# One division for both heads of a pair, behind the slot's maxima: a decoder layer on one core

## The chip, the cores and the metric

The kernel runs on one core of a Trainium2 chip. The metric is device time in microseconds (us) for one execution of the whole program. Three timed runs of the kernel before gave 662.83, 663.38 and 667.53 us; the median is 663.38 us. One more execution was recorded by the hardware profiler; it took 661.71 us.

## The reference

One decoder layer on x of 4 batches, 1024 rows and 256 features, in float32. Three blocks are added to x one after the other, each on a layer norm of x:

```python
x = x + attn(layernorm(x))          # 16 heads of 16, local: a chunk of 128 rows sees itself and the chunk before, causal
x = x + xattn(layernorm(x), ctx)    # 16 heads of 16, 77 keys from ctx, mask, biases
x = x + ffn(layernorm(x))           # 704 wide, inputs and weights rounded to 8 bits, silu(gate) * up
```

Both attentions are softmax attentions: `softmax(q k^T / 4) v`, then a product with an output matrix. The division of the softmax is by the sum of the exponentials of a row.

## The kernel before, in words

**Layout.** The kernel takes the attention in eight jobs: S0 S1 S2 X0 S3 X1 X2 X3. S is the self attention and X the cross attention of one batch. In a job, g (2) is one half of the features, that is eight heads; these eight heads are two groups of four, o = 0 and o = 1. The four heads of a group (j) lie in the four quarters of 32 partitions, so that TensorE works on four heads at once. A pair of heads here is o = 0 and o = 1 of the same g and j. hf (2) is a half of the 1024 rows. u counts the units of one (g, o): four for S (256 rows each), two for X (512 rows each). A branch is taken at run time, and here the arm runs in which all rows of the mask are alike (`alike` is true).

**Softmax without a second pass.** For each unit the scores are computed twice. First with rows on the partitions (`sc_n`, L735 for S, L750 for X), four PSUM banks, and VectorE takes the row maxima out of them (`maxima`: L765 for S, eight pairs of instructions per unit; L776 for X, four instructions per unit). The maxima are transposed (`ps_mx`, L787), copied (L791) and sent by DMA into a spare row of q (L801). Five units later (`LEAD = 5`) the scores are computed again with keys on the partitions and the maxima already subtracted (`sc_t`, L827 and L856, four banks), and ScalarE takes the exponential (L837, L859). For S, GpSimd sets the masked half to zero (L841).

**Weighted values and the division.** `weighted_values` multiplies the exponentials with the values (`ps_av`, L871 and L881), one bank per (g, o, hf); a column of ones in the values makes the row's sum. VectorE transposes the bank in 32x32 blocks into `o_sb` (L895), which frees the bank. `normalise` takes the reciprocal of the 16 sums (L903) and multiplies 16x16 values (L905) into `aN`, at the place of head o. After o = 1, `by_features` transposes `aN` in 32x32 blocks into `aT` (L917), from which `out_project` (`ps_op`, L306) later computes the product with the output matrix, which VectorE adds to x (L935).

**The order.** It is written out by hand, slot by slot (L1231 to L1290); each engine works through its own list in that order. In a slot come:

1. the weighted values that are due, each with transposition, reciprocal, product and, for o = 1, the transposition to `aT` (L1254 to L1258);
2. usually one task of TensorE from a list ordered by due time: `project` (`ps_p`), `values` (`ps_v`), `normed_T` (`ps_t`, then the copies L341 and L343), `out_project`, preparations of weights;
3. work beside it, mostly VectorE's: statistics of the layer norm (L192, L194), quantising of weights (L608 to L618), the largest values for the next block (L966);
4. `put_maxima`, where a group's maxima were completed one slot before;
5. `sc_n` and the maxima of the unit five ahead;
6. `sc_t`, the exponentials and masks of the unit of this slot.

In a stretch of S units a slot with weighted values is followed by one without; in a stretch of X units each slot has some.

**Banks.** The eight PSUM banks go round in the order in which they are asked for. The first bank that a slot asks for is the one that, eight requests earlier, was the first `sc_n` bank of the slot before (that slot's last eight banks are four `sc_n` and four `sc_t`). So the weighted values at the head of a slot start once VectorE has taken the first bank's maxima in the slot before.

**Buffers.** `o_sb` has one buffer of 128x512, `aN` two, `aT` three, the scratch output `junk` of the maxima two.

Of the kernel before, what the change touches and what calls it, by code (L numbers as in the profile page):

```python
# [9 lines left out]
F32 = mybir.dt.float32  # L10
# [4 lines left out]
ALU = mybir.AluOpType  # L15
# [3 lines left out]
P = 128  # L19
# [6 lines left out]
def decoder_layer(  # L26
# [32 lines left out]
    nc = tc.nc  # L59
# [5 lines left out]
    H, HD, SL = 16, 16, 32  # L65
    NP = 2
    NS = 2
# [3 lines left out]
    HS = S // NH  # L71
# [9 lines left out]
    small = ctx.enter_context(tc.tile_pool(name="small", bufs=3))  # L81
# [120 lines left out]
    with ExitStack() as att:  # L202
# [64 lines left out]
        def slot_of(v, h):  # L267
            return v.rearrange("p h e -> p (h e)")[:, h * (HD + 1) : h * (HD + 1) + SL]
# [7 lines left out]
        def next_of(key, tiles):  # L276
            turn[key] += 1
            return tiles[(turn[key] - 1) % len(tiles)]
# [7 lines left out]
        class Job:  # L286


            def __init__(self, kind, b):
                self.kind, self.b = kind, b  # L290
                self.leads = (kind, b) == ("S", 0)
                self.st = {}
                self.xn, self.xnT, self.vs, self.q, self.k = {}, {}, {}, {}, {}
                self.aN, self.aT, self.mx, self.pts, self.av = {}, {}, {}, {}, {}

            def branch(self):
                twin = copy.copy(self)
                for k, v in vars(self).items():
                    if isinstance(v, dict):
                        setattr(twin, k, dict(v))  # L300
                return twin
# [119 lines left out]
        def attention(alike):  # L421
# [5 lines left out]
            work = arm.enter_context(tc.tile_pool(name="work", bufs=2))  # L427
# [388 lines left out]
            def weights(job, g, o, u):  # L816
# [34 lines left out]
                else:  # L851
# [5 lines left out]
                    for j in range(NJ):  # L857
                        pt = work.tile([SK, HS], F32, name="ptx", tag="pt", bufs=16)
                        nc.scalar.activation(pt, banks[j][:SK], AF.Exp)  # L859
                        job.pts[g, o, j, u] = pt  # L860

            def weighted_values(job, g, o, hf):
                ps = bank("ps_av")
                heads = [2 * NJ * g + 2 * j + o for j in range(NJ)]
                if job.kind == "S":
                    t0 = hf * HT
                    for kb in range(max(t0 - 1, 0), t0 + HT):

                        a0, a1 = max(kb, t0), min(kb + 2, t0 + HT)
                        for j in range(NJ):  # L870
                            nc.tensor.matmul(  # L871
                                ps[j * SL : (j + 1) * SL, (a0 - t0) * P : (a1 - t0) * P],
                                slot_of(job.vs[kb // 2][:, kb % 2], heads[j]),
                                job.pts[g, o, j, kb // 2][:, kb % 2, a0 - kb : a1 - kb, :],
                                start=(kb == max(t0 - 1, 0)),
                                stop=True,
                                skip_group_check=True,
                            )
                else:
                    for j in range(NJ):  # L880
                        nc.tensor.matmul(  # L881
                            ps[j * SL : (j + 1) * SL, :],
                            slot_of(vx[:, job.b], heads[j]),
                            job.pts[g, o, j, hf],
                            start=True,
                            stop=True,
                        )

                if job is jobs[-1] and (g, o, hf) == (NP - 1, NS - 1, NH - 1):
                    job.av[g, o, hf] = next_of("xnT", xnTs)[  # L890
                        :, 0, :
                    ]
                else:
                    job.av[g, o, hf] = work.tile([P, HS], F32, name="o_sb", tag="o_sb", bufs=1)
                nc.vector.transpose(job.av[g, o, hf], ps)  # L895

            def normalise(job, g, o, hf, tail):

                if o == 0:
                    job.aN[g, hf] = work.tile([P, HS], F32, name="aN", tag="aN", bufs=2)  # L900
                on = job.av[g, o, hf].rearrange("p (s e) -> p s e", e=SL)
                rec = small.tile([P, HS // SL, 1], F32, name="rec")
                nc.vector.reciprocal(rec, on[:, :, HD : HD + 1])  # L903
                aN = job.aN[g, hf].rearrange("p (s e) -> p s e", e=SL)
                (nc.gpsimd if tail else nc.vector).tensor_tensor(  # L905
                    aN[:, :, o * HD : (o + 1) * HD],
                    on[:, :, 0:HD],
                    rec.to_broadcast([P, HS // SL, HD]),
                    ALU.mult,
                )  # L910

            def by_features(job, g, o, hf):

                if o == NS - 1:
                    if g == 0:
                        job.aT[hf] = work.tile([P, NC, HS], F32, name="aT", tag="aT", bufs=3)
                    nc.vector.transpose(job.aT[hf][:, g, :], job.aN[g, hf])  # L917
# [181 lines left out]
            jobs = [leading.branch()]  # L1099
# [15 lines left out]
            values_of, added, puts, early, late = {}, {}, {}, {}, {}  # L1115
# [24 lines left out]
            for j, job in enumerate(jobs):  # L1140
# [4 lines left out]
                for hf in range(NH):  # L1145
# [41 lines left out]
                    g = NP - 1  # L1187
# [43 lines left out]
            for slot in range(first, last):  # L1231
                present["slot"] = slot
                now = units[slot] if 0 <= slot < N else None
                ahead = units[slot + LEAD] if 0 <= slot + LEAD < N else None
                for fn, args in early.get(slot, ()):
                    fn(*args)
                tail = slot >= N - LEAD
                if slot == N:

                    pair = values_of[slot] + values_of.pop(slot + 1)  # L1240
                    for args in pair:
                        weighted_values(*args)
                        normalise(*args, tail)
                    for args in pair:
                        by_features(*args)
                    while beside:
                        t = min(beside, key=lambda t: t[1:3])
                        beside.remove(t)
                        t[4](*t[5])
                        while after:  # L1250
                            after.pop(0)()
                    last_project(jobs[-1])
                else:
                    for args in values_of.get(slot, ()):  # L1254
                        weighted_values(*args)
                        normalise(*args, tail)
                        if not tail:
                            by_features(*args)  # L1258
                spent = 0.0
                cap = 1.35 if now and ahead else 2.3  # L1260
                while t := next_in(tasks, slot, spent, cap):
                    spent += t[3]
                    fn, args = t[4:]
                    fn(*args)
                    if fn is out_project:
                        job, hf, t2 = args
                        if job.kind == "X" and t2 == HT // 2 - 1:
                            third_norm(job.b, hf, slot)
                spent = 0.0
                while t := next_in(beside, slot, spent, 1.2):  # L1270
                    spent += t[3]
                    t[4](*t[5])
                if tail and slot < N:
                    for args in values_of.get(slot, ()):
                        by_features(*args)
                for args in puts.get(slot, ()):
                    put_maxima(*args)
                if ahead:
                    max_bias(*ahead)
                    if now and now[0].kind == "X" and not alike:  # L1280
                        weight_bias(*now)
                    maxima(*ahead)
                if now:
                    if alike or not (ahead and now[0].kind == "X"):
                        weight_bias(*now)
                    weights(*now)
                for fn, args in late.get(slot, ()):
                    fn(*args)
                while after:
                    after.pop(0)()  # L1290
# [264 lines left out]
        with tc.If(rows_alike != 0, preferred_fallthrough_block=True) as branch:  # L1555
            attention(True)
            feed_forward()
        with branch.Else():
            attention(False)
            feed_forward()  # L1560
# [49 lines left out]
```

## Time and profile before

| what | value |
|---|---|
| timed runs, median | 663.38 us |
| profiled execution | 661.71 us |
| its span | 660.0 us |
| TensorE busy / VectorE busy, 0 to 548 us (attention) | 525.30 / 447.35 us |
| TensorE busy / VectorE busy, 548 to 660 us (feed forward) | 82.13 / 94.19 us |
| mean granted TensorE clock | 0.986 |

The span is the time between the first and last instruction; the execution took 1.7 us more. PE is TensorE's matmuls, PEld its weight loads, DVE is VectorE, ACT ScalarE, POOL GpSimd, SP the engine that issues DMAs. In a line of the groups of instructions stand the line of the kernel, engine, operation, output <- input, shapes, the count, the busy time in us and the mean time of one in ns, and then the idle time of the engine just before them with what ended it. In the timeline stand the start and the length in us, and in brackets how long the engine had been idle and what it waited for. Busy matmuls are pipelined, four heads beside each other, so their lengths overlap.

### The profile page before, as it was taken

How to read it: one execution, taken by the hardware profiler on the slowest of the kernel's cores; microseconds unless marked ns; L12 is line 12 of the kernel's file. 1: busy time of each engine (PE TensorE's matmuls, PEld its weight loads, DVE VectorE, ACT ScalarE, POOL GpSimd, SP SyncE). 2: the span in 40 equal slices, each digit the busy share in tenths (PEclk: the TensorE clock that was granted, in tenths of full speed). 3: DMA queues.
4: the chain of work that ended last, by engine and by line, in shares of the span. 5: the costliest groups of instructions: out<-in, count | busy, mean ns of one | idle time of the engine just before them, and what ended most of it. 6: DMA issues, size and time to landing. Idle time of an engine off the chain costs nothing.

```text
span 660.0 us, 20192 instructions
## 1 busy us (share of the span) xinstructions
PE 607.4 (92%) x7862; PEld 347.5 (53%) x7862; DVE 541.5 (82%) x1915; ACT 366.8 (56%) x672; POOL 268.6 (41%) x522
## 2 busy tenths in 40 slices
PE   9899999999999989989999999999999997878774
PEld 6456556566565655544456655544434345334564
DVE  5778878788689798578997986888878787799896
ACT  2365655644656536455565365447466565698392
POOL 3164633645227487440064866526601141111032
PEclk9999999999999999799999999999999999899898
DMA  8100100000000000000000000000000110000057
GB/s 289 51 5 16 38 4 20 4 5 23 3 28 12 11 12 14 5 22 18 5 11 11 13 26 28 5 4 6 4 4 6 35 65 17 1 0 1 1 96 164
DMA packets 19293, 17.93 MB, mean 27 GB/s; under 512 B 3190, under 2 KB 18551, under 8 KB 19191
## 3 DMA queue, kind: packets, MB, share of 16 engines
q1 hardware_dynamic: 16999, 14.74, 7.0%
q0 software_dynamic: 1904, 1.84, 2.1%
q8 instruction: 64, 1.05, 0.6%
q14 instruction: 38, 0.31, 0.1%
q10 hardware_dynamic: 288, 0.00, 0.0%
HBM read 9.47 MB, written 6.03 MB: 23 GB/s over the span
## 4 chain that ended last, share of the span: by engine, by line
PE 56%; DVE 30%; ACT 6%; issue 6%; POOL 1%; DMA 1%; DVEq 0%; ACTq 0%
PE ps_p L306 11%; PE ps_av L871 7%; PE sc_n L735 7%; PE sc_t L827 6%; PE ps_op L306 6%; DVE junk L765 5%; PE ps_av L881 3%; DVE o_sb L895 3%; PE ps_v L306 3%; DVE bnst L192 2%; PE sc_n L750 2%; PE sc_t L856 2%; DVE aT L917 2%; PE ps_idle L117 2%; DVE x L935 2%
## 5 line engine op out<-in xcount | busy, mean ns | idle before, releaser
L765 DVE CUSTOM_DVE_ANT_0 junk<-sc_n,cboth 128x256 bf16<-128x256 f32 (+1 forms) x512 | 172.7, 403 | 33.1 <-PE sc_n L735 32.7
L837 ACT ACTIVATE pt<-sc_t 128x512 f32<-128x512 f32 (+1 forms) x256 | 125.4, 577 | 84.3 <-PE sc_t L827 83.1
L841 POOL TENSOR_SCALAR_AFFINE_SELECT pt<-pt 128x256 f32<-128x256 f32 x256 | 101.7, 407 | 113.1 <-ACT pt L837 102.9
L859 ACT ACTIVATE ptx<-sc_t 77x512 f32<-77x512 f32 x128 | 65.2, 596 | 36.1 <-PE sc_t L856 36.1
L827 PE MATMUL sc_t<-shared 32*128 32x256 f32 (+1 forms) x1024 | 79.8, 371 | 2.9 <-DMA shared<-mxT 1.8
L735 PE MATMUL sc_n<-shared 32*128 32x256 f32 (+1 forms) x1024 | 75.1, 387 | 2.7 <-ACT shared L377 1.2
L322 POOL TENSOR_SCALAR xn<-x,mv,rs 128x256 f32<-128x256 f32 x56 | 69.7, 1251 | 0.0
L827 PEld LDWEIGHTS sc_t<-shared 32*128 32x128 f32 x1024 | 61.6, 186 | 11.0 <-ACT mxT L791 2.7
L160 POOL TENSOR_SCALAR ve<-mv 128x4 f32<-128x4 f32 x20 | 4.6, 232 | 153.3 <-DVE mv L194 153.3
L895 DVE STREAM_TRANSPOSE o_sb<-ps_av 128x512 f32<-128x512 f32 x63 | 45.0, 714 | 24.4 <-PE ps_av L871 15.3
L306 PE MATMUL ps_p<-shared,w_s 128*32 128x512 f32 x512 | 60.9, 595 | 3.3 <-DVE mx L776 1.7
L735 PEld LDWEIGHTS sc_n<-shared 32*128 32x128 f32 x1024 | 46.1, 184 | 33.3 <-DVE mx L765 12.6
L871 PE MATMUL ps_av<-pt,vt 128*32 128x256 f32 (+1 forms) x1152 | 60.3, 353 | 3.0 <-DVE mx L765 2.6
L776 DVE TENSOR_REDUCE mx<-sc_n 128x4 f32<-128x308 f32 x128 | 51.8, 467 | 8.7 <-PE sc_n L750 8.5
L871 PEld LDWEIGHTS ps_av<-pt,vt 128*32 128x32 f32 x1152 | 35.5, 112 | 31.9 <-issue 6.9
L765 DVE DVE_READ_ACCUMULATOR2_ANT mx<- 128x1 f32 x512 | 42.9, 84 | 0.0
L856 PE MATMUL sc_t<-shared,kx 32*77 32x512 f32 x256 | 42.8, 598 | 0.0
L377 ACT ACTIVATE shared<-ps_p 128x512 f32<-128x512 f32 x32 | 19.1, 597 | 38.7 <-PE ps_p L306 38.7
L881 PE MATMUL ps_av<-ptx,vx 77*32 77x512 f32 x256 | 36.0, 605 | 4.8 <-DVE mx L776 3.1
L750 PEld LDWEIGHTS sc_n<-kx,shared 32*128 32x128 f32 x1024 | 31.7, 186 | 10.2 <-DVE mv L194 1.7
L750 PE MATMUL sc_n<-kx,shared 32*128 32x77 f32 x1024 | 36.4, 277 | 0.0
L1423 ACT ACTIVATE act<-pg,gsc 128x512 f32<-128x512 f32 x44 | 29.2, 687 | 11.6 <-PE pg L1408 8.9
(200 smaller groups left out, 990.7 us busy)
## 6 DMA issues: line engine op xcount, KB each, us to landing
x<-in_x_dram SPq DMA_DIRECT2D x8, 512.0 KB
out_dram<-shared SPq DMA_DIRECT2D x9, 256.0 KB
shared<-mxT SPq DMA_DIRECT2D x128, 4.0 KB
out_dram<-x SPq DMA_DIRECT2D x7, 256.0 KB
out_dram<-shared POOLq DMA_DIRECT2D x7, 256.0 KB, 4.5
w_s<-in_L_attn_w_qkv_dram SPq DMA_DIRECT2D x2, 384.0 KB
raw_d<-in_L_ffn_w_down_dram SPq DMA_DIRECT2D x2, 352.0 KB
raw_f<-in_L_ffn_w_gate_dram SPq DMA_DIRECT2D x5, 128.0 KB
```

What stands on the lines that cost most here:

```text
L306: nc.tensor.matmul(out[r], lhsT[:, r], rhs, skip_group_check=True, **on)
L322: eng.tensor_scalar(xn, xb[job.b][:, t, :], job.st[hf].mv[:, i, 0:1], job.st[hf].rs[:, i : i + 1], ALU.subtract, ALU.mult,)
L735: nc.tensor.matmul(banks[j][:, (i + 1) * 2 * P - n : (i + 1) * 2 * P], q[r, t * P : (t + 1) * P], k[r, k0 * P : k0 * P + n], start=True, s ...
L750: nc.tensor.matmul(banks[j][:, i * SK : (i + 1) * SK], q[r, t * P : (t + 1) * P], k[r, :], start=alike, stop=alike or i == HT - 1,)
L765: nc.vector.tensor_tensor_reduce(out=junk[:, 2 * P - n :], in0=banks[j][:, (i + 1) * 2 * P - n : (i + 1) * 2 * P], in1=cboth[:, 2 * P - n ...
L827: nc.tensor.matmul(banks[j][:, w : w + n], k[r, t * P : (t + 1) * P], q[r, t * P : t * P + n], start=True, stop=True,)
L837: nc.scalar.activation(pt.rearrange("p i a q -> p (i a q)")[:, :w], banks[j][:, :w], AF.Exp)
L841: nc.gpsimd.affine_select(out=pt[:, :, 0, :], in_=pt[:, :, 0, :], compare_op=ALU.is_ge, fill=0.0, base=0, pattern=[[0, 2], [1, P]], channe ...
L856: nc.tensor.matmul(banks[j][:SK], k[r, :], q[r, s], start=alike, stop=True)
L859: nc.scalar.activation(pt, banks[j][:SK], AF.Exp)
L871: nc.tensor.matmul(ps[j * SL : (j + 1) * SL, (a0 - t0) * P : (a1 - t0) * P], slot_of(job.vs[kb // 2][:, kb % 2], heads[j]), job.pts[g, o, ...
L895: nc.vector.transpose(job.av[g, o, hf], ps)
```

## The change

For all jobs but the last (X3) and only in the arm that runs, the two transposed banks of a pair are kept (`o_sb` now holds both, 128 x 2 x 512, in two buffers), and `normalise` and `by_features` are not called in the slot's first step any more. In their place `normalise_pair` takes one reciprocal of 2x16 sums and makes one product of 2x16x16 values for both heads, and `by_features` transposes the result. Both are called in the slot of o = 1, at its end: behind the maxima of that slot and behind the issue of `sc_t`, ahead of everything of the next slot. `aN` of a pair has one buffer. X3 still divides head by head; its `aN` and `o_sb` are the two halves of one buffer, so the two row halves no longer share one `o_sb`. The buffers of `junk` stay two. On TensorE, ScalarE and GpSimd no instruction is added, removed or moved.

```diff
+                self.pair = {}
...
+            def apart(job):
+                return job is jobs[-1] or not alike
+
             def weighted_values(job, g, o, hf):
...
-                else:
+                elif not alike:
                     job.av[g, o, hf] = work.tile([P, HS], F32, name="o_sb", tag="o_sb", bufs=1)
+                else:
+                    if o == 0:
+                        job.pair[g, hf] = work.tile(
+                            [P, NS, HS], F32, name="o_sb", tag="o_sb", bufs=2
+                        )
+                    job.av[g, o, hf] = job.pair[g, hf][:, 0 if apart(job) else o, :]
                 nc.vector.transpose(job.av[g, o, hf], ps)
 
             def normalise(job, g, o, hf, tail):
 
                 if o == 0:
-                    job.aN[g, hf] = work.tile([P, HS], F32, name="aN", tag="aN", bufs=2)
+                    if alike:
+                        job.aN[g, hf] = job.pair[g, hf][:, 1, :]
+                    else:
+                        job.aN[g, hf] = work.tile([P, HS], F32, name="aN", tag="aN", bufs=2)
...
+            def normalise_pair(job, g, hf):
+
+                aN = job.aN[g, hf] = work.tile([P, HS], F32, name="aN", tag="aN", bufs=1)
+                on = job.pair[g, hf].rearrange("p o (s e) -> p o s e", e=SL)
+                rec = small.tile([P, NS, HS // SL, 1], F32, name="rec2", bufs=1)
+                nc.vector.reciprocal(rec, on[:, :, :, HD : HD + 1])
+                nc.vector.tensor_tensor(
+                    aN.rearrange("p (s o d) -> p o s d", o=NS, d=HD),
+                    on[:, :, :, 0:HD],
+                    rec.to_broadcast([P, NS, HS // SL, HD]),
+                    ALU.mult,
+                )
...
                     for args in values_of.get(slot, ()):
                         weighted_values(*args)
+                        if not apart(args[0]):
+                            continue
                         normalise(*args, tail)
                         if not tail:
                             by_features(*args)
...
                     weights(*now)
+                for job, g, o, hf in values_of.get(slot, ()):
+                    if o == NS - 1 and not apart(job):
+                        normalise_pair(job, g, hf)
+                        by_features(job, g, o, hf)
                 for fn, args in late.get(slot, ()):
```

More of the change, by code (lines that the diff above doesn't have):

```diff
@@ L892, in weighted_values @@
                     ]
-                else:
-                    job.av[g, o, hf] = work.tile([P, HS], F32, name="o_sb", tag="o_sb", bufs=1)
+                elif not alike:
+                    job.av[g, o, hf] = work.tile([P, HS], F32, name="o_sb", tag="o_sb", bufs=1)
+                else:
+                    if o == 0:
[3 more added lines that the diff above has]
+                    job.av[g, o, hf] = job.pair[g, hf][:, 0 if apart(job) else o, :]
                 nc.vector.transpose(job.av[g, o, hf], ps)
```

## The prediction

> **What bounds the kernel now.** I read the busy shares first, then the chain that ended last, the waits, the groups of VectorE, and the timeline around the places that the change touches.
>
> ```profile
> PE 607.4 (92%) x7862; PEld 347.5 (53%) x7862; DVE 541.5 (82%) x1915; ACT 366.8 (56%) x672; POOL 268.6 (41%) x522
> ...
> PE 56%; DVE 30%; ACT 6%; issue 6%; POOL 1%; DMA 1%; DVEq 0%; ACTq 0%
> ```
>
> TensorE is the bound, but VectorE holds 30% of the chain: TensorE takes its PSUM banks back from VectorE's maxima and has little spare time when it does. In the list of waits, TensorE's waits for maxima (`mx` L765 and L776) add up to 15.0 us before 548 us. The largest kind is the weighted values at the head of a slot:
>
> ```profile
> PE ps_av L881 <- DVE mx L776: 3.1, 10, 0.9
> PE ps_av L871 <- DVE mx L765: 2.6, 6, 1.1
> ```
>
> **What the change removes.** From the groups of VectorE:
>
> ```profile
> L895 DVE STREAM_TRANSPOSE o_sb<-ps_av 128x512 f32<-128x512 f32 x63 | 45.0, 714 | 24.4 <-PE ps_av L871 15.3 <-PE ps_av L881 7.0 <-POOL aN L905 1.2
> ...
> L905 DVE TENSOR_TENSOR aN<-o_sb,rec 128x256 f32<-128x256 f32 x57 | 25.1, 440 | 2.0
> L917 DVE STREAM_TRANSPOSE aT<-aN 128x512 f32<-128x512 f32 x32 | 22.7, 709 | 1.8 <-POOL aN L905 0.7
> ...
> L903 DVE RECIPROCAL rec<-o_sb 128x16 f32<-128x16 f32 x63 | 16.0, 254 | 2.1
> ```
>
> Seven jobs have 28 pairs (2 g, 2 hf). Each loses two reciprocals (0.25 us each) and two products (0.43, median) and gets one of each. The trace has no pair-wide form. Bounds: the reciprocal between 0.25 (one of now) and 0.51 (two); the product between 0.43 and 0.85. I take 0.27 and 0.69: SBUF products of 512 elements take 0.692 (L1538) against 0.425 for 256, so about 1 ns per element on top of a fixed part. A pair then costs 0.27 + 0.69 + 0.71 (L917) = 1.67 us, in place of 0.51 + 0.85 + 0.71 = 2.07: 0.40 less, 11 us of VectorE over 28 pairs. With the small steps between them (0.03) and the early start of the next instruction (0.08), the pair holds VectorE's list for 1.66 us.
>
> **Where it goes.** In the slot of o = 0, 0.68 us leaves the front; in that of o = 1, 1.39 us. But the 1.66 us stands ahead of everything VectorE has in the next slot: copies and additions, statistics, and the next maxima. On the others' queues (SP, POOL, ACT) nothing is moved.
>
> **The gain.** One slot shows it:
>
> ```profile
> 283.38 0.71 DVE L917 STREAM_TRANSPOSE aT<-aN 128x512 f32<-128x512 f32 x1
> ...
> 284.68 1.62 DVE L776 TENSOR_REDUCE mx<-sc_n 128x4 f32<-128x308 f32 x4
> ...
> 285.21 1.92 PE L306 MATMUL ps_p<-shared,w_s 128*32 128x512 f32 x16 [1.67 <-DVE mx L776]
> ```
>
> The scores were ready at 282.84; the maxima start only at 284.68, behind reciprocal, product, `aT` and 0.72 us of quantising, and TensorE stands for 1.67 us. Without the three, they start at about 283.1: 1.4 us of the wait go, net of what the pair brings into the next slot. I went through all of TensorE's gaps before 548 us and kept those whose VectorE run, without a break, holds a division in front of the maxima, never moving the maxima ahead of the end of `sc_n`: 1.4 here, 0.77 at 70.4, 0.58 at 332.7, 0.5 at 240, 0.4 at 61.8, 0.34 at 372.1, 0.31 at 154.4, 0.3 at 426.2, 0.24 at 111.3 and 197.7, 0.19 at 382.4, four waits of 0.16 in cross slots (0.6), and 0.3 in X3, where `o_sb` waited 1.2 us for GpSimd. Sum 6.2 us. Elsewhere VectorE already waits for the scores (32.7 us idle ahead of L765 in its group), and earlier division buys nothing.
>
> **The loss: the next slot's maxima.** A self-attention slot without weighted values is short:
>
> ```profile
> 81.94 1.61 PE L735 MATMUL sc_n<-shared 32*128 32x256 f32 x13
> ...
> 82.49 0.69 DVE L341 COPY shared<-ps_t 128x512 f32<-128x512 f32 x1
> ...
> 83.49 0.42 DVE L765 CUSTOM_DVE_ANT_0 junk<-sc_n,cboth 128x256 bf16<-128x256 f32 x1 [0.31 <-PE sc_n L735]
> ...
> 84.56 1.72 PE L871 MATMUL ps_av<-pt,vt 128*32 128x256 f32 x32
> ```
>
> The pair of 77.8 belongs to the slot before, whose maxima last from 79.73 to 82.58 (2.85 us). VectorE's spare time up to the next maxima is 0.31 us. New order: pair up to 84.16, the copy up to 84.77, maxima from 84.77 instead of 83.49. The weighted values need the first bank, which comes free 0.80 us after the maxima start (332.68 - 331.88 where TensorE waits for it). 83.49 + 0.80 = 84.29, so there is 0.27 of slack now; new 85.57 instead of 84.56: TensorE waits 1.01 us. Behind it wait, in order, all of the slot's projections and scores, so it is on the path.
>
> In general, from the end of one `sc_n` to the next TensorE takes about 0.9 (`sc_t`) + 1.9 (one task) + 1.1 = 4.0 us; VectorE would need 2.85 + 1.66 plus 0 to 2.2 of its side work. Only where a slot has two tasks does the pair find room. The same working for each pair (positions of maxima and `sc_n` from the timeline, slack between 0.03 and 0.35) gives these waits in us:
>
> S0 0.17, 1.01, 0.97, 0.61; S1 0.72, 0, 1.00, 1.08; S2 0.90, 1.53, 0.10, 0; S3 1.00, 1.46, 0, 0.74: together 11.3. Cross attention has shorter maxima (1.6) and weighted values in each slot, so mostly room: X0 0, 0.82, 0, 1.11; X1 0.71 at its last; X2 0.10: together 2.7. Sum 14.0 us.
>
> **The loss: `aT` comes late.** Most output products start 6 us or more after their `aT`. Three do not: at 415.15 (2.1 us after), 464.84 (2.9) and 507.75 (2.0).
>
> ```profile
> 505.05 0.71 DVE L917 STREAM_TRANSPOSE aT<-aN 128x512 f32<-128x512 f32 x1
> ...
> 507.23 1.63 DVE L776 TENSOR_REDUCE mx<-sc_n 128x4 f32<-128x308 f32 x4
> ...
> 507.75 1.93 PE L306 MATMUL ps_op<-wo_x,aT 128*32 128x256 f32 x32 [0.17 <-DVE mx L776]
> ```
>
> Here the maxima, held by L966, which itself waits for ScalarE, move from 507.23 to about 506.6; they end at 508.2, `aT` at 509.85, so the product starts at 509.9: 2.15 later. The other two: 1.8 and 0.96. Sum 4.9 us.
>
> **The sum.** 14.0 + 4.9 - 6.2 = 12.7 us. The profiled execution took 661.7 us (span 660.0 and 1.7 around it), so 674.4 by its own clock. The median of the runs shown is 1.7 above it: 676.1, predicted as **676 us**. With the pair's bounds (0.28 less, 0.40 more) at the 20 places that wait, the sum moves by -5.6 and +8: 670 to 684.
>
> **The clock.** A row says that waits can cost twice:
>
> ```profile
> 263.14:266.55 3.41, 2.09 (x38) 1.59 (x39) 1.63 (x4) 1.50 (x2) 0.82 (x2) 1.00 0.04 12
> 266.55:269.97 3.42, 3.42 (x30) 2.13 (x34) 0.00 (x0) 2.06 (x4) 1.22 (x3) 0.50 0.02 5
> ```
>
> (start:end, length, busy of PE, PEld, DVE, ACT, POOL, then the granted clock.) One gap of 1.30 us, at 264.15, was followed by two such stretches at a clock of 0.50, which is 3.4 us of TensorE time lost. The gap of 1.67 at 283.5 was not. So I put new spells at nothing in the sum and at 3.4 us each in the range; two gaps grow above 1.7 us. The Trainium skill (TensorE: Matmul & The Clock Gate, "HAM oscillation — how this bites in real kernels") says that only gaps over about 3.4 us bring the clock down. By it no wait of this change costs any clock, and the upper end would be 684; the trace here speaks against it.
>
> **Rivals.**
> *Given back (no change).* A stall of TensorE lets ScalarE, VectorE and DMA run ahead, and later waits shrink. For it: gaps at 245.4 (1.11), 265.5 (1.30), 361.8 (0.83), 396.0 (0.48), 464.0 (0.63), 488.8 (0.88), 506.5 (0.91) and 315.3 (0.50), 6.6 us, come from chains partly outside the division. Against: most of them start on TensorE itself and move along. 676 - 6.6 = 669.5.
> *Faster.* The pair fits behind the maxima, since the first bank is not what the next slot waits for or the slot is longer than I read; then only the gains stay, 6.2 us, and up to 3.1 more of the waits for L776: 663.4 - 9.3 = 654. It decides from the point where 1.66 us and the side work fit between the end of the maxima and the end of the next `sc_n`. Against: that time is some 1.2 us in short slots.
> *More half-clock spells.* Two more: 676 + 6.8 = 683.
>
> **Chances.** Forecast (670 to 684) 0.62; given back 0.22, near 669; faster 0.10; more spells 0.06. A change of 1%, 6.6 us, is about what a measurement of this kernel can tell from none. Faster by over 1% 0.10, within 1% 0.23, slower 0.67. The range 660 to 685 leaves out the faster rival and part of the clock's.
>
> **What would show it.** Right: 28 fewer reciprocals and products; TensorE's waits for L765 and L776 up from 15 to some 23 us, at weighted values two slots behind a pair; three new waits of output products for `aT`, about 2 us; the gap at 285 gone. VectorE's busy time down by 11 us while the span grows. Wrong: the maxima of short slots start at the end of `sc_n` as now, or output products wait nowhere.

## The result and the profile after

The kernel after takes **680.4 us** (median of six runs, 678.73 to 685.4) against 663.35 us (662.38 to 667.53) before. The ratio is 1.027, with a 95% interval of 1.0239 to 1.0301. The profiled execution took 678.73 us with a span of 677.0 us, 17.0 us more than before.

Line numbers below are those of the kernel after: the maxima are L766 (S) and L777 (X), the weighted values L875 (S) and L885 (X), the transposition that frees their bank L905, the pair's reciprocal, product and transposition L930, L931 and L943, the output product and the projections L307, the copy of the transposed norm L342, the addition to x L961, `sc_t` L828, the masks L842.

First the page of the profile after: busy times of the engines, and the shares of the chain that ended last.

```profile
PE 615.8 (91%) x7857; PEld 349.6 (52%) x7862; DVE 533.1 (79%) x1859; ACT 367.2 (54%) x672; POOL 272.2 (40%) x522
...
PE 56%; DVE 30%; ACT 6%; issue 6%; POOL 1%; DMA 1%; DVEq 0%; ACTq 0%
```

VectorE has 56 instructions fewer and is busy 8.4 us less, yet the span grew by 17.0 us, and VectorE's share of the chain stayed at 30%. TensorE has the same work (five of its records are missing in the feed forward, x7857 in place of x7862); its recorded busy time grew by 8.4 us, 7.7 of them in attention (525.30 to 532.98).

The list of what TensorE waited for in the kernel after, up to the end of attention (565 us); the columns are the total, the number of times, and the longest, in us:

```profile
PE ps_av L875 <- DVE mx L766: 8.2, 13, 1.3
PE ps_op L307 <- DVE aT L943: 4.2, 3, 1.6
PE ps_av L885 <- DVE mx L777: 3.2, 5, 1.5
PE sc_t L828 <- DVE shared L342: 2.8, 3, 0.9
PE sc_t L828 <- DMA shared<-mxT: 2.0, 2, 1.2
PE ps_op L307 <- DVE mx L766: 1.9, 4, 0.8
PE sc_t L828 <- DVE x L961: 1.4, 2, 0.8
```

Weighted values of S wait for maxima 8.2 us where they waited 2.6. Three waits for `aT` are new (4.2 us), and so are five waits of `sc_t` for a copy or an addition of VectorE (2.8 + 1.4 = 4.2 us). Waits for maxima over the whole list are 16.3 us, where they were 15.0, since the wait of 1.67 us at 285 us is nearly gone (0.14 left, at 289.22) and the other waits of projections for maxima have gone too.

That makes 1.3 + 4.2 + 4.2 = 9.7 us more waiting on VectorE. With 7.7 us more busy time in attention and 0.7 us less of other waits it is 16.7, nearly the 17.0 of the span. The busy time grew for two reasons that can be seen. Stretches at half clock in attention took 13.65 us after against 6.83 before; TensorE was busy for 12.7 us of them, where it was 6.8, and half of the difference, 3.0 us, is an estimate of what the clock cost. And where TensorE stops in the middle of a run of `sc_t`, the matmuls on the two sides of the stop no longer overlap, so that the records cover more time: outside the half-clock stretches `sc_t` for S takes 81.0 us where it took 77.8. The other 1.5 us of the 7.7 were not placed.

One slot without weighted values shows the mechanism. The timeline of the kernel after (start, length, engine, instruction; in brackets the idle time and what ended it):

```profile
79.96 1.61 PE L736 MATMUL sc_n<-shared 32*128 32x256 f32 x13
...
80.89 0.86 DVE L931 TENSOR_TENSOR aN<-o_sb,rec 128x512 f32<-128x512 f32 x1
...
81.78 0.71 DVE L943 STREAM_TRANSPOSE aT<-aN 128x512 f32<-128x512 f32 x1
...
82.42 0.65 DVE L342 COPY shared<-ps_t 128x512 f32<-128x512 f32 x1
82.99 0.41 DVE L766 CUSTOM_DVE_ANT_0 junk<-sc_n,cboth 128x256 bf16<-128x256 f32 x1
...
83.13 1.13 PE L828 MATMUL sc_t<-shared 32*128 32x256 f32 x12 [0.92 <-DVE shared L342]
...
84.19 1.72 PE L875 MATMUL ps_av<-pt,vt 128*32 128x256 f32 x32
```

This is the slot that the prediction worked through (there at 81.94). The pair of the slot before stands first in VectorE's list, then the copy, then the maxima. From the start of this run of `sc_n` to the weighted values it was 84.56 - 81.94 = 2.62 us before; now it is 84.19 - 79.96 = 4.23. The slot became 1.61 us longer, against 1.01 predicted. The longer pair (1.86 us, below, and not 1.67) makes 0.2 of the difference. The other 0.4 comes by another path: TensorE stops at `sc_t`, whose next bank is held by the late copy, and the weighted values can only follow when `sc_t` is through. Had they waited for the first bank's maxima alone, they would have started at 82.99 + 0.80 = 83.79. The list of waits shows 0.92 of the 1.61 us. The other 0.7 is time that the records of the broken run of `sc_t` cover: 81.20 to 82.21 and 83.13 to 84.26, 2.14 us together, where it was 1.44.

The pair itself, in the groups of VectorE, one shape a line (count, busy us, mean ns):

```profile
L931 DVE TENSOR_TENSOR aN<-o_sb,rec 128x512 f32<-128x512 f32 x28 | 22.4, 800 | 1.0
L943 DVE STREAM_TRANSPOSE aT<-aN 128x512 f32<-128x512 f32 x28 | 19.9, 711 | 1.0
...
L930 DVE RECIPROCAL rec<-o_sb 128x32 f32<-128x32 f32 x28 | 9.7, 347 | 0.0
```

It takes 0.347 + 0.800 + 0.711 = 1.86 us, not 1.67. Two divisions head by head and a transposition took 2 x 0.254 + 2 x 0.440 + 0.709 = 2.10 by the means of before. So the merge saves 0.24 us for a pair and not 0.40; over 28 pairs that is 6.7 of the 8.4 us.

One of the three late output products, in the timeline after:

```profile
425.57 0.35 DVE L930 RECIPROCAL rec<-o_sb 128x32 f32<-128x32 f32 x1
...
425.95 0.90 DVE L931 TENSOR_TENSOR aN<-o_sb,rec 128x512 f32<-128x512 f32 x1
426.88 0.71 DVE L943 STREAM_TRANSPOSE aT<-aN 128x512 f32<-128x512 f32 x1
...
427.64 2.79 PE L307 MATMUL ps_op<-wo_s,aT 128*32 128x256 f32 x24 [1.64 <-DVE aT L943]
```

What follows it, in a table by stretches of the kernel after (start:end, length, busy time and count of PE, PEld, DVE, ACT, POOL, granted clock, share of DMA, GB/s):

```profile
423.90:427.49 3.59, 2.05 (x28) 1.01 (x24) 3.49 (x9) 2.21 (x6) 2.79 (x5) 1.00 0.04 10
427.49:430.90 3.41, 3.26 (x36) 1.53 (x36) 0.47 (x2) 0.00 (x0) 3.41 (x5) 0.50 0.02 4
```

The gap of 1.64 us, from 426.00 to 427.64, leaves TensorE busy for 2.05 us of 3.59, and from 427.49 on the granted clock is 0.50. At 523.06 the clock falls in the midst of the gap of 1.39 us (522.43 to 523.83), 2.1 us behind another of 1.54 that is a wait for maxima. The two other stretches, at 273.89 and 407.01, stand behind waits of `sc_t` for a DMA. The second of these shows how little it can take:

```profile
403.60:407.01 3.41, 2.62 (x39) 1.75 (x36) 1.64 (x4) 1.22 (x2) 2.93 (x3) 1.00 0.12 39
```

Here the gap was 0.75 us.

### The profile page after: what moved, and what is told of

Its sections match the earlier page's. It is cut to its first block, busy times and chain, and to the rows that moved or that the text cites. A ratio compares the mean times of both kernels' runs of the same rounds, so it can differ in the third digit from the quotient of the medians.

```text
span 677.0 us, 20134 instructions
## 1 busy us (share of the span) xinstructions
PE 615.8 (91%) x7857; PEld 349.6 (52%) x7862; DVE 533.1 (79%) x1859; ACT 367.2 (54%) x672; POOL 272.2 (40%) x522
## 4 chain that ended last, share of the span: by engine, by line
PE 56%; DVE 30%; ACT 6%; issue 6%; POOL 1%; DMA 1%; DVEq 0%; ACTq 0%
PE ps_p L307 10%; PE ps_av L875 8%; PE ps_op L307 7%; PE sc_n L736 6%; DVE junk L766 6%; PE sc_t L828 5%; PE ps_v L307 3%; PE sc_n L751 3%; PE ps_av L885 3%; PE sc_t L857 3%; DVE aT L943 2%; DVE aN L931 2%; DVE mx L777 2%; DVE bnst L192 2%; PE pg L1440 2%
## 5 line engine op out<-in xcount | busy, mean ns | idle before, releaser
L766 DVE CUSTOM_DVE_ANT_0 junk<-sc_n,cboth 128x256 bf16<-128x256 f32 (+1 forms) x512 | 172.7, 402 | 47.6 <-PE sc_n L736 47.1
L842 POOL TENSOR_SCALAR_AFFINE_SELECT pt<-pt 128x256 f32<-128x256 f32 x256 | 102.6, 410 | 123.5 <-ACT pt L838 113.6
L828 PE MATMUL sc_t<-shared 32*128 32x256 f32 (+1 forms) x1024 | 84.2, 375 | 7.2 <-DVE shared L342 2.8
L828 PEld LDWEIGHTS sc_t<-shared 32*128 32x128 f32 x1024 | 63.6, 186 | 17.4 <-DVE shared L342 4.0
L323 POOL TENSOR_SCALAR xn<-x,mv,rs 128x256 f32<-128x256 f32 x56 | 72.6, 1302 | 0.0
L875 PE MATMUL ps_av<-pt,vt 128*32 128x256 f32 (+1 forms) x1152 | 60.4, 354 | 8.5 <-DVE mx L766 8.2
L307 PE MATMUL ps_p<-shared,w_s 128*32 128x512 f32 x512 | 60.9, 596 | 0.4 <-ACT shared L344 0.2
L905 DVE STREAM_TRANSPOSE o_sb<-ps_av 128x512 f32<-128x512 f32 x63 | 44.4, 704 | 21.4 <-PE ps_av L875 15.5
L777 DVE TENSOR_REDUCE mx<-sc_n 128x4 f32<-128x308 f32 x128 | 52.0, 469 | 9.0 <-PE sc_n L751 8.7
L875 PEld LDWEIGHTS ps_av<-pt,vt 128*32 128x32 f32 x1152 | 35.8, 112 | 37.9 <-DVE mx L766 9.1
L857 PE MATMUL sc_t<-shared,kx 32*77 32x512 f32 x256 | 44.2, 598 | 0.1
L766 DVE DVE_READ_ACCUMULATOR2_ANT mx<- 128x1 f32 x512 | 42.5, 83 | 0.0
L885 PE MATMUL ps_av<-ptx,vx 77*32 77x512 f32 x256 | 36.0, 605 | 3.6 <-DVE mx L777 3.2
L961 DVE TENSOR_TENSOR x<-x,ps_op 128x512 f32<-128x512 f32 x28 | 19.1, 682 | 23.6 <-PE ps_op L307 23.5
```

The source lines that it names most:

```text
L307: nc.tensor.matmul(out[r], lhsT[:, r], rhs, skip_group_check=True, **on)
L323: eng.tensor_scalar(xn, xb[job.b][:, t, :], job.st[hf].mv[:, i, 0:1], job.st[hf].rs[:, i : i + 1], ALU.subtract, ALU.mult,)
L766: nc.vector.tensor_tensor_reduce(out=junk[:, 2 * P - n :], in0=banks[j][:, (i + 1) * 2 * P - n : (i + 1) * 2 * P], in1=cboth[:, 2 * P - n ...
L777: nc.vector.tensor_reduce(mx[:, j, tiles * u : tiles * (u + 1)], banks[j].rearrange("p (i k) -> p i k", i=tiles), AX.X, ALU.max, negate=True,)
L828: nc.tensor.matmul(banks[j][:, w : w + n], k[r, t * P : (t + 1) * P], q[r, t * P : t * P + n], start=True, stop=True,)
L842: nc.gpsimd.affine_select(out=pt[:, :, 0, :], in_=pt[:, :, 0, :], compare_op=ALU.is_ge, fill=0.0, base=0, pattern=[[0, 2], [1, P]], channe ...
```

## The experiments

The kernel before ran beside each group of experiments: 662.59 us (median of 11 runs) beside the first four, 663.12 us (17 runs) beside the others.

**Theory.** Each place where the pair stands ahead of maxima, copies or additions that TensorE's banks wait for costs the pair's length less VectorE's spare time there; three late `aT` and some half clock come on top. **Rivals:** the merged form itself is what costs; the late `aT` and the half clock behind them are most of it; the place hardly matters. **Open sizes:** why the product takes 0.80 us, and how much of the gain in front is real. An edit shifts the lines of what stands behind it, so go by the tile's name in what follows: the maxima of S are the first of two lines of `mx`, those of X the second, and likewise for `ps_av`.

### e1_front: the merged form, at the old place

```diff
                         weighted_values(*args)
                         if not apart(args[0]):
+                            if args[2] == NS - 1:
+                                normalise_pair(args[0], args[1], args[3])
+                                by_features(*args)
                             continue
...
-                for job, g, o, hf in values_of.get(slot, ()):
-                    if o == NS - 1 and not apart(job):
-                        normalise_pair(job, g, hf)
-                        by_features(job, g, o, hf)
```

> The pair is still divided once, but in the first step of the slot of o = 1, where the two divisions were before; nothing of it stands behind the maxima. Theory A (the pair delays the next slot's maxima, and TensorE waits for their first bank): the waits of weighted values for maxima fall from 11.4 us (8.2 + 3.2) to about 6, the three waits for aT (4.2 us) go, time 662 to 668. Theory B (late aT and the half-clock spells behind it are most of it): the same here, 662 to 668. Theory C (the merged form itself is what costs, wherever it stands): 672 or more.

Measured: 668.39 us (666.82 to 669.97), ratio 1.0106 [1.0071, 1.0141]. TensorE's waits in this kernel, in the same columns:

```profile
PE ps_av L885 <- DVE mx L777: 3.1, 7, 1.1
PE ps_p L307 <- DVE mx L766: 2.8, 4, 1.2
PE ps_av L875 <- DVE mx L766: 2.6, 6, 1.1
PE ps_p L307 <- DVE mx L777: 2.0, 1, 2.0
```

The weighted values of S wait 2.6 us, as before the change, and there is no wait for `aT`. So about 12 of the 17 us belong to the place, late `aT` and clock included. The time is 0.4 us above the range that the theory gave and 3.6 below that of the merged form as the cause. The rest, 5.8 us, comes with the division of both heads in one slot: in the slot of o = 1 the whole pair (0.35 + 0.70 + 0.71 = 1.76 us at this place) now stands where one division and a transposition stood (0.25 + 0.43 + 0.71 = 1.39), and what leaves the slot of o = 0 seems to have been little waited for. The waits of `ps_p` show it: 2.8 against 1.4, and the one at 285 us grew from 1.7 to 2.0. Waits for maxima are 18.2 us in all, against 15.0, and half clock in attention took 10.2 us, against 6.8.

### e2_two_behind: four instructions instead of two, at the new place

```diff
-                if o == 0:
+                if o == 0 and apart(job):
...
             def normalise_pair(job, g, hf):
-                aN = job.aN[g, hf] = work.tile([P, HS], F32, name="aN", tag="aN", bufs=1)
...
+                job.aN[g, hf] = work.tile([P, HS], F32, name="aN", tag="aN", bufs=1)
+                for o in range(NS):
+                    normalise(job, g, o, hf, False)
```

> At the place behind the maxima stand two reciprocals and two products instead of one of each; the transposition as in the changed kernel. A pair then holds VectorE for 0.51 + 0.85 + 0.71 = 2.07 us without GpSimd beside it, against 0.35 + 0.80 + 0.71 = 1.86 us measured. Theory A: each tenth of a us ahead of the next maxima counts at some 20 places, so 0.2 more makes 4 us: 683 to 688. Theory B: the same as the changed kernel, 679 to 682, plus 0.6 at three output products. Theory C: faster than the changed kernel, 670 to 678.

Measured: 687.61 us (685.65 to 692.04), ratio 1.0402 [1.0348, 1.0455]. Waits of weighted values for L766 rise from 8.2 to 9.4 us, those of `sc_t` for the copy from 2.8 to 3.0 and for the addition from 1.4 to 2.2. The longer the block behind the maxima, the longer the waits: 7.2 us of time for one more reciprocal and one more product at each of 28 pairs, a block of 0.49 + 0.96 + 0.71 = 2.16 us in place of 1.86. Not all of that is waiting: half clock in attention took 20.5 us, against 13.65. The time lies in the theory's range (683 to 688). At this place the merge does pay.

### e3_three_front: only the three pairs with a late `aT` in front

```diff
+            def soon(job, g, o, hf):
+                return alike and (g, o, hf) == (NP - 1, NS - 1, 0) and job in jobs[4:7]
...
                         weighted_values(*args)
+                        if soon(*args):
+                            normalise_pair(args[0], args[1], args[3])
+                            by_features(*args)
...
-                    if o == NS - 1 and not apart(job):
+                    if o == NS - 1 and not apart(job) and not soon(job, g, o, hf):
```

> As the changed kernel, but the three pairs whose output product follows within 3 us (S3, X1, X2, each with g = 1, hf = 0) are divided in the first step of their slot. Theory A: the three waits for aT (4.2 us) go and with them the half-clock spells at 427 and 523 us (1.7 us each): 672 to 677; the waits of weighted values stay. Theory B: nearly all of the loss goes: 662 to 668.

Measured: 678.61 us (674.37 to 680.58), ratio 1.025 [1.0197, 1.0302]. The first lines of TensorE's waits in this kernel:

```profile
PE ps_av L878 <- DVE mx L766: 8.2, 13, 1.3
PE sc_t L828 <- DVE shared L342: 2.8, 3, 0.9
PE ps_av L888 <- DVE mx L777: 2.7, 5, 1.1
```

The waits for `aT` are gone, the others are nearly as they were, and the median is only 1.8 us lower, which the two ranges of runs don't tell from nothing; it is above the theory's 672 to 677, too. The span of the profiled execution fell by 1.2 us, not by 4.2: TensorE is busy 1.7 us more (617.5 against 615.8). Half clock in attention took 13.65 us again, with stretches at 252, 276 and 522 us, so the one near 523 comes without a wait for `aT` as well. The rival that the late `aT` explain most of it falls (it gave 662 to 668).

### e4_next_slot: pairs of S0, S1 and of all g = 0 one slot further back

```diff
+            put_off = {}
...
+                for job, g, hf in put_off.pop(slot, ()):
+                    normalise_pair(job, g, hf)
+                    by_features(job, g, NS - 1, hf)
                 for job, g, o, hf in values_of.get(slot, ()):
                     if o == NS - 1 and not apart(job):
+                        if g == 0 or job in jobs[:2]:
+                            put_off.setdefault(slot + 1, []).append((job, g, hf))
+                            continue
```

> The pairs of S0 and S1 and all pairs of g = 0 are divided one slot later, behind the maxima of the short slot; the others as in the changed kernel. Theory A: the waits of weighted values two slots behind these pairs (about 1.1 us each, 13 waits and 8.2 us in all for self attention) mostly go, but the division now stands ahead of the transposition and the side work of a slot with weighted values, which has 0.3 to 1 us of room less than it needs in places: 670 to 677, with waits at other slots. Theory B: aT is later still, time 680 or more.

Measured: 666.3 us (664.11 to 668.69), ratio 1.0057 [1.003, 1.0084]. The slot shown above, in the timeline of this kernel:

```profile
79.71 1.61 PE L736 MATMUL sc_n<-shared 32*128 32x256 f32 x13
...
80.26 0.69 DVE L342 COPY shared<-ps_t 128x512 f32<-128x512 f32 x1
...
81.25 0.42 DVE L766 CUSTOM_DVE_ANT_0 junk<-sc_n,cboth 128x256 bf16<-128x256 f32 x1 [0.31 <-PE sc_n L736]
...
82.33 1.72 PE L875 MATMUL ps_av<-pt,vt 128*32 128x256 f32 x32
```

The same three instructions now stand behind the maxima of the slot without weighted values. Copy and maxima are ahead of them again, and from `sc_n` to the weighted values it is 2.62 us, as before the change. Its waits:

```profile
PE ps_op L307 <- DVE aT L943: 4.2, 3, 1.6
PE ps_av L875 <- DVE mx L766: 3.6, 6, 1.3
PE ps_av L885 <- DVE mx L777: 2.5, 5, 0.9
```

The waits of `sc_t` for the copy and the addition are gone, those for `aT` are as they were, and weighted values of S wait 3.6 us instead of 8.2. The same instructions in the same number cost 14 us less, one slot later for 18 of the 28 pairs. So the cost lies in what stands behind the block, and a longer way to `aT` costs nothing at these pairs. The expectation had 670 to 677: it feared the work of the next slot with weighted values, and that had more room than it gave.

### e5_no_masks: without GpSimd's masks

```diff
-                        nc.gpsimd.affine_select(
-                            out=pt[:, :, 0, :],
...
-                        )
                         job.pts[g, o, j, u] = pt
```

> The changed kernel without GpSimd's masks of the self attention (the 256 operations of L842): what leaves out the causal zeros, so its output isn't the reference's; only the length of VectorE's operations is of interest. In the changed kernel the product of a pair took 691 to 693 ns in the nine places where GpSimd ran nothing beside it and 700 to 1120 ns where it did (mean 824 beside the masks). If GpSimd is the cause: about 692 ns wherever no other operation of GpSimd (xn, bias) lies beside it, and a mean below 740. If the place or the form is the cause (the same data, the same pattern): the mean stays at 800.

Measured: one run, 677.23 us. The pair's product in the groups of this kernel:

```profile
L922 DVE TENSOR_TENSOR aN<-o_sb,rec 128x512 f32<-128x512 f32 x28 | 19.6, 702 | 1.0
```

And in the view of the tile, with minimum, median and maximum in ns and the first and last start in us:

```profile
L922 DVE TENSOR_TENSOR aN<-o_sb,rec x28: 691/692/886, 70.5 to 527.3; 128x512 f32<-128x512 f32 x28
```

In the kernel after the same view gives 691, 778 and 1120. Without the masks 26 of 28 products take 691 to 694 ns; the two others stand beside GpSimd's bias (886) and its norm (762). So the product has its estimated 0.69 us where GpSimd leaves it alone, and GpSimd's work beside it makes the 0.80; the place or the form would have kept the mean at 800 ns. The time hardly moved: 0.1 us for each of 28 pairs is 2.8 us at most.

### e6_aT_behind: the division as before, only the transposition to `aT` behind the maxima

This edit is made in the kernel before, so its lines in the trace are those of before.

```diff
                         normalise(*args, tail)
-                        if not tail:
+                        if not tail and args[0] is jobs[-1]:
                             by_features(*args)
...
                     weights(*now)
+                for args in () if tail else values_of.get(slot, ()):
+                    if args[0] is not jobs[-1]:
+                        by_features(*args)
```

> The kernel before, with its two divisions per pair in front, and only the transposition to aT (0.71 us) behind the slot's maxima. Theory A: 0.71 us is ahead of the next maxima in place of 1.86; the short slots have 0 to 0.5 us of room, so some ten of them lose 0.2 to 0.7, three output products wait about 0.6 less than in the changed kernel, and the waits at 285 and 332 us shrink by 0.7: 663 to 669. If what is behind the maxima cost nothing as such, and the division's form did: 660 to 662.

Measured: 661.56 us (656.25 to 663.92, ten runs), ratio 0.9962 [0.9933, 0.9992]. From TensorE's waits in this kernel:

```profile
PE ps_av L881 <- DVE mx L776: 3.7, 8, 1.5
PE ps_av L871 <- DVE mx L765: 3.4, 9, 1.1
```

The block behind the maxima is 0.71 us now, not 1.86. Weighted values of S wait 0.8 us more than before and those of X 0.6 more; output products wait 1.0 us for `aT`; elsewhere, in front, waits for maxima fall by more: all waits for maxima are 13.0 us against 15.0, and 14.0 with those for `aT`. Most slots can take 0.7 us. The theory, which gave 663 to 669 us, priced so short a block too high; the time lies in the other range, 660 to 662, of a block that costs nothing there. It does not follow that a longer block is free there: the pair at this place gave 680 us, and 668 in front.

### e7_mix: each pair at its cheapest place

From the timelines of before, after and e4, each pair was given one of three places: head by head as before ("each"), behind its own slot's maxima ("behind"), or behind the next slot's ("next").

```diff
-            def apart(job):
-                return job is jobs[-1] or not alike
+            def place(job, g, hf):
+                k = jobs.index(job)
+                if k == 7 or not alike:
+                    return "each"
+                if k < 2 or k in (2, 4) and g == 0 or (k, g, hf) == (3, 1, 1):
+                    return "next"
+                if (k, g) in ((2, 1), (5, 0), (6, 0)) or (k, g, hf) == (3, 1, 0):
+                    return "behind"
+                return "each"
+
+            def apart(job, g, hf):
+                return place(job, g, hf) == "each"
...
+            put_off = {}
...
+                for job, g, hf in put_off.pop(slot, ()):
+                    normalise_pair(job, g, hf)
+                    by_features(job, g, NS - 1, hf)
                 for job, g, o, hf in values_of.get(slot, ()):
-                    if o == NS - 1 and not apart(job):
+                    if o == NS - 1 and not apart(job, g, hf):
+                        if place(job, g, hf) == "next":
+                            put_off.setdefault(slot + 1, []).append((job, g, hf))
+                            continue
```

> Each pair where the traces so far show it cheapest: one division behind the next slot's maxima for S0, S1, the first halves (g = 0) of S2 and S3, and the last pair of X0; one division behind the slot's own maxima for the second half of S2, the third pair of X0 and the first halves of X1 and X2; all others as in the kernel before. Theory A: the gain of 5.5 us that the run with pairs one slot later had over the kernel before at the end of S2 stays, X0 and S3 give back about 1: 657 to 660. If the gains at single slots are taken back later: 662 to 664.

Measured: **654.75 us** (652.95 to 657.15), ratio 0.987 [0.983, 0.9911]: faster than both kernels. The busy times on its page:

```profile
PE 605.0 (93%) x7862; PEld 346.5 (53%) x7862; DVE 534.9 (82%) x1875; ACT 366.9 (56%) x672; POOL 272.4 (42%) x522
```

And the waits of weighted values in its list (L895 is X here and L885 S):

```profile
PE ps_av L895 <- DVE mx L777: 2.8, 8, 0.9
PE ps_av L885 <- DVE mx L766: 2.3, 5, 1.1
```

No output product waits for `aT`, and waits for maxima are 11.1 us in all, against 15.0 before: 3.9 less. TensorE is busy 2.4 us less. These two make 6.3 of the 7.6 us of span. Attention ends 6.3 us earlier (the last `ps_op` at 541.3 in place of 547.6); the feed forward, which the edit doesn't touch, is 1.2 us shorter and had 7.7 us at half clock in place of 11.2. The time is below both ranges of the expectation.

### e8_first_bank: the pairs of e4, inside the next slot's maxima

The pair stands between the maxima of the first bank and those of the other three.

```diff
                 for j in range(NJ):
+                    while j == 1 and put_off:
+                        late_job, late_g, late_hf = put_off.pop(0)
+                        normalise_pair(late_job, late_g, late_hf)
+                        by_features(late_job, late_g, NS - 1, late_hf)
...
+            put_off = []
...
                     if o == NS - 1 and not apart(job):
+                        if g == 0 or job in jobs[:2]:
+                            put_off.append((job, g, hf))
+                            continue
```

> The same pairs as in the run with pairs one slot later, but the division stands in the next slot's maxima, behind the first bank's and ahead of the other three's. If it is the first bank that the weighted values wait for, they no longer wait (as there, 3.6 us of waits in self attention), and the second bank's task (1.7 to 1.9 us later on TensorE) waits about 0.6 us at some twelve places: 668 to 675. If it is not the first bank but the whole of the maxima that is late: like the changed kernel, 678 to 681.

Measured: 674.35 us (673.02 to 675.35), ratio 1.0154 [1.0103, 1.0205]. The first lines of TensorE's waits in this kernel:

```profile
PE ps_p L307 <- DVE mx L770: 4.4, 9, 0.7
PE ps_op L307 <- DVE aT L947: 4.2, 3, 1.6
PE ps_av L879 <- DVE mx L770: 3.6, 6, 1.3
```

Weighted values of S wait exactly as in e4 (3.6 us, 6 times), although three of four banks get their maxima 1.8 us later. So they do wait for the first bank alone where they wait for maxima, as the prediction had it. But the projections behind them take the later banks, and now they wait: 4.4 us, in nine waits that e4 does not have. The time is in the range that the first bank gave (668 to 675).

## Why the prediction was right, and which terms were off

The forecast, 676 us and slower, came out within its own bounds (670 to 684), 4.3 us low. By its steps:

- **The mechanism: right, but one path was left out.** The pair at a slot's end makes the next slot's maxima late where that slot is short. The slot worked through was priced at 1.01 us and became 1.61 longer; e4 takes the block out of that place and the 1.61 is gone; e2 makes the block longer and the waits grow; e8 shows that the first bank is what the weighted values wait for. In the slot worked through, though, it was the copy behind the pair that held TensorE longest, through `sc_t`.
- **The faster rival: wrong for this change, right for another place.** The pair doesn't fit behind its own slot's maxima in short slots. Behind the next slot's (e4) and with a choice for each pair (e7) it does, and then there is a gain.
- **The rival "given back": not seen.** Its 669 us did not come, and two of the larger gaps that it named, at 265.5 and 361.8 (1.30 and 0.83 us), are still there (1.23 us at 272.57, 0.84 at 367.67).
- **The reciprocal, "between 0.25 and 0.51, I take 0.27": mis-sized.** It takes 0.347 us. The trace of before held the row that tells it: L611 takes 165 ns for one element, L903 254 for 16, so about 6 ns for each further one, and 350 for 32.
- **The product, "0.69": right alone, wrong beside GpSimd.** It takes 0.691 to 0.694 us where GpSimd is idle and 0.80 on the mean (e5). The row that the estimate came from, L1538, has none of GpSimd's masks, biases or norms beside it.
- **These two terms together** make the pair 0.19 us longer at some 20 places that wait, 3.8 us by the prediction's own working; they are also why VectorE's busy time fell by 8.4 us and not by 11.
- **"Waits for L765 and L776 up from 15 to some 23 us": wrong as a sign to look for.** They are 16.3. The same lateness stands under another name where a copy or an addition is held up with the maxima: five waits of `sc_t`, 4.2 us, and some 3.2 us more in the records of its broken runs. The prediction named copies and additions as what stands behind the pair, but followed only the maxima from there to TensorE.
- **Late `aT`, 4.9 us in three places: right**, 4.2 us in three (1.64, 1.20, 1.39). In e3 they are gone and the median is 1.8 us lower, not 4.2.
- **The gap at 285 us gone: right**, 1.67 to 0.14.
- **The clock, "new spells at nothing in the sum": mis-sized.** Attention spends 6.8 us more at half clock, by the estimate above 3.0 us of time. The trace here agrees with the row that the prediction showed and not with the rule of the Trainium skill (TensorE: Matmul & The Clock Gate, "HAM oscillation — how this bites in real kernels"), "no PE-idle gaps >~3.4µs", as the prediction read it: stretches at a clock of 0.50 followed gaps of 0.75 to 1.64 us.

Put together by the lists, in us: waits and broken runs behind maxima, copies and additions, with the gains in front taken off, 1.3 + 4.2 + 3.2 - 0.7 = 8.0, where the prediction had 14.0 - 6.2 = 7.8; late `aT` 4.2 for 4.9; the clock 3.0 for nothing; 1.5 of busy time not placed. So the clock is the term that was missing. That 8.0 and 7.8 agree is partly luck: with the pair at its measured length the prediction's working would have given 7.8 + 3.8 = 11.6, so it priced the waits some 3.5 us too high, and that covered the pair that it had too short. Which of the waits were too high stays open. e6 points the same way: behind a block of 0.71 us they were smaller than its expectation gave.

One thing could have been read beforehand. The Trainium skill (SBUF — State Buffer, "SBUF: two separate sides") says that VectorE and GpSimd share a port pair, and that a VectorE instruction with two inputs in SBUF and a GpSimd instruction that reads SBUF shut each other out: the one that starts first has the pair for its whole length. The runs agree that the two hinder each other: the product, which has two such inputs, takes 692 ns alone and 824 ns on the mean in the six places where only masks of 0.41 us stood beside it. Four products of e5 that began in the last 0.14 us of a norm instruction kept 692 to 693 ns, and it was GpSimd's next one that took 1.66 to 1.73 us in place of 1.23. The runs don't agree that one is shut out whole: at 477.52 us the product ran wholly beside a norm instruction (477.18 to 478.40) and took 746 ns. Transpositions, with one input, keep their 711 to 712 ns.

## What to carry to other kernels

Work that is moved behind something on an in-order engine stands ahead of everything that comes next there: price it at its new neighbours, through every bank that they hold, and look one slot further before settling on a place. A merge of two instructions saves little by itself (here 0.24 us for a pair), and that counts only where their time is waited for; here the same three instructions gave 680 us at one place, 666 with 18 of the 28 pairs at the next, and 655 when each pair was placed by its own slack, eight of them divided head by head as before. The lateness may show at another instruction than the one forecast, so compare the time between two fixed instructions, and not the list of waits alone: in the slot shown they say 1.61 and 0.92 us.

## What was not expected of the hardware

- A product on VectorE with both inputs in SBUF can stretch from 0.69 to as much as 1.12 us when GpSimd works beside it, while VectorE's transposition does not stretch (711 to 712 ns in 28 of 28, 15 of them with GpSimd at work beside them).
- A reciprocal in float32 costs about 6 ns for each further element of a partition: 164 ns for 1, 254 for 16, 347 for 32. The transposition takes 0.71 us for 512 elements, 1.4 ns each on the average.
- Stretches of 3.41 us at half clock came behind short gaps of TensorE: 1.64, 1.23 and even 0.75 us in the kernel after, 1.30 in the kernel before. But a gap of 1.67 us (before, 283.54) and one of 1.31 (after, 214.43) brought none. Nor does the busy time of the 3.41 us ahead settle it: TensorE was busy for 2.15, 2.62, 1.87 and 1.50 us ahead of the four stretches of the kernel after, and for 2.10 us from 212.45 on, where none came. What decides stays open. The places of the stretches moved with the edits (e3: 252, 276 and 522 us in place of 274, 407, 427 and 523).
